# Window attention's probabilities transposed in two halves of the TensorE array, and the second image's first loads issued together

## The chip, the cores and the metric

The kernel runs on one core of a Trainium2 chip. The core has five engines that work side by side: TensorE (PE, matmuls; its weight loads are listed apart as PEld), VectorE (DVE), ScalarE (ACT), GpSimd (POOL) and SyncE (SP), which here issues nearly all the DMAs. The metric is the device time of one execution in microseconds. Before the change it was 1659.49 us, the median of three runs that took from 1656.48 to 1663.47 us.

## The reference

The input `x` is 16 images of 56 x 56 tokens with 128 channels, in float32. Two layers follow each other, both with a residual:

```python
# layer 0: shifted-window attention; 64 windows of 7 x 7 = 49 tokens, 4 heads of 32
x = x + L0_conv(_gn(x))            # group norm, qkv, dots * scale + bias + mask,
                                   # softmax over 49 keys, times v, w_out, b_out
# layer 1, on the 3136 tokens of an image in a row
t = t + L1_attn(_ln_t(t))          # causal linear attention: elu(q)+1, elu(k)+1, running sums
t = t + L1_ffn(_ln_t(t))           # batch norm, then y[t] = sigmoid(wx[t] + y[t-1] @ V.T)
```

The change lies in the first layer: in a window, `softmax(q k^T + bias + mask) @ v`.

## The kernel before, in words

The kernel goes over the 16 images, b = 0 to 15, and works on several at once. An image is cut twice. For the window attention it is eight rows of eight windows (`window_row`, u = 0 to 7, NW = 8 windows of WT = 49 tokens). For the linear attention and what follows it is six groups of 512 tokens and one of 64 (`token_group`, g = 0 to 6). The recurrent part of the feed-forward layer comes behind all images, from about 1500 us to the end, and the change doesn't touch it.

One window row is a chain of steps over the engines:

- ACT gathers the windows (`gather_windows`, L851); PE projects q and k (L864) and the values (L885); ACT copies them out.
- PE computes the scores (L909): 32 small matmuls per row, each with 32 rows of the array (a head) and 49 columns. The four heads lie on four strips of 32 rows. Head h's scores go to partitions 64 x (h mod 2) on, so that a partition half holds one head of a pair.
- DVE adds the mask and takes the maximum (L920, L932), POOL subtracts it (L935), ACT takes the exponential (L945), DVE sums (L949, L951), POOL scales (L954).
- PE transposes the probabilities (`turn`, L964). `p_buf` holds two heads in its two partition halves, rows 0 to 48 and rows 64 to 112, with two windows padded to 64 columns each beside each other. One transpose takes both halves at once: 113 rows, 128 columns. Eight transposes do a window row.
- ACT copies the transposed probabilities to `pT` (`turn_out`, L974), 904 elements per partition, of which the columns between the two heads are padding.
- PE multiplies with the values (`mix`, L983): 32 small matmuls, each with 49 rows in one of the two halves of the array and 32 columns. ACT writes the result to `oT` (`mix_out`, L1018).

The transposes, the scores and the mix each use one of two PSUM tiles, `pairs`, of two banks.

A float32 matmul appears in the trace as two matmul instructions, so 32 small matmuls are 64; a transpose appears as one.

The images' data come in twice. `load` brings the tokens as rows (`xt_bufs`, L323), for the residual. For images 1 to 15 `load_turned` and `load_blocks` bring the same image in four parts (q = 0 to 3) of blocks of 32 channels to `spare[0]` (L335); DVE turns these 32 x 32 blocks (`turn_rows`, L683), which gives the image with channels on partitions. Statistics (L755) and the group norm follow, and only then can the image's first window be gathered. Image 0 is transposed on PE instead (L649).

The order of the instructions on every engine is written by a planner (`Plan`), which runs in the kernel's own Python. Each step names its engine, a cost, a lag to its end, the steps it comes after and the buffers that it takes and drops. The planner plays the steps through with these numbers, forwards and backwards, many times, and emits them by start time in the best order it finds. The engines then run their queues in that order and wait on semaphores. A step whose `tiles` is set is one that uses a part of the array: having begun with such a step, the planner prefers another one nearby, and it adds 0.1 to the first of them (`SWITCH`). Before, `scores` and `mix` are marked so. SP's DMAs, too, stand in the planned order, so a DMA that waits holds those behind it.

In the planner's model the four parts of an image's blocks come after each other: each part's step names the part before it. This is a rule of the plan alone; no semaphore comes from it, since the parts write to different partitions.

## Time and profile before

| what | us |
|---|---|
| median of three runs | 1659.49 |
| the profiled execution | 1664.5 |
| its span on the core | 1661.4 |
| PE busy in the span | 1615.4 |
| DVE busy | 1398.1 |
| POOL busy | 1272.0 |
| ACT busy | 1183.5 |

The page of the profile gives the busy time of each engine, the chain of work that ended last followed back from the end, and the groups of instructions that cost most. In a group the first number is the time in which at least one of its instructions was under way, the second the mean duration of one in ns. On PE these durations overlap, since matmuls are pipelined: a step's price is better read in the order of time, from its first start to the first start of the step behind it. A stretch's busy times are read against its length. The granted clock is the share of TensorE's full clock, 1.00 for most of this execution.

### The profile page before, as it was taken

The page shows a single profiled execution, that of the slowest core. Times are in us where ns is not written, and L with a number is a line of the kernel's source. Part 1 is how long each engine was busy: PE and PEld are TensorE (multiplying, and loading weights), DVE is VectorE, ACT ScalarE, POOL GpSimd, SP SyncE. Part 2 cuts the span into 40 slices and gives each one's busy share as a digit, 9 for nine tenths or more (in the row PEclk, how much of TensorE's full clock was granted, in tenths as well). Part 3 has the DMA queues.
Part 4 walks back from the last instruction along what each step waited for, and adds up shares of the span by engine and source line. Part 5 has one row for each costly group of instructions (what it writes and reads, how often), then busy time and mean ns, then how long its engine had stood idle before and what let it go on. Part 6 is the DMA issues. An engine that isn't in the chain of part 4 may idle for free.

```text
span 1661.4 us, 63385 instructions
## 1 busy us (share of the span) xinstructions
PE 1615.4 (97%) x25458; PEld 1308.8 (79%) x25459; DVE 1398.1 (84%) x3044; ACT 1183.5 (71%) x3156; POOL 1272.0 (77%) x2154
## 2 busy tenths in 40 slices
PE   7899999999999999999999999999999999999997
PEld 6678787887878887878888778878888887876876
DVE  5779987897989888987979798978898786757997
ACT  5577776777777777777677777767677776766765
POOL 6788978897989898888989889878889786770000
PEclk9999999999999999999999999999999999999999
DMA  5486767677677768586766777776755655558999
GB/s 137 109 186 158 192 151 172 187 167 208 154 204 166 199 153 206 149 208 169 194 165 156 204 168 196 167 191 156 196 148 155 159 160 147 190 183 342 403 419 379
DMA packets 776720, 322.03 MB, mean 194 GB/s; under 512 B 400481, under 2 KB 760161, under 8 KB 774625
## 3 DMA queue, kind: packets, MB, share of 16 engines
q1 hardware_dynamic: 774832, 317.10, 69.9%
q8 instruction: 202, 3.31, 0.9%
q10 hardware_dynamic: 1584, 0.79, 0.2%
q14 instruction: 102, 0.83, 0.2%
HBM read 171.54 MB, written 146.24 MB: 191 GB/s over the span
## 4 chain that ended last, share of the span: by engine, by line
PE 69%; POOL 8%; DVE 7%; SPq 5%; DMA 5%; issue 3%; ACT 2%; DVEq 0%; POOLq 0%; ACTq 0%
PE bank L864 8%; PE bank L1269 8%; PE bank L885 5%; PE pair L909 5%; PE state_bank L1412 4%; PE pair L964 4%; PE pair L1401 4%; PE bank L1317 4%; PE pair L1404 4%; PE bank L1502 4%; PE bank L1372 4%; PE pair L983 4%; SPq L1072 4%; PE bank L1234 4%; PE z_buf L1785 2%
## 5 line engine op out<-in xcount | busy, mean ns | idle before, releaser
L954 POOL TENSOR_TENSOR p_buf<-p_buf,rc 128x784 f32<-128x784 f32 x128 | 194.4, 1519 | 42.7 <-DVE rc L951 14.2
L1269 PE MATMUL bank<-xnT,awc_sb 128*128 128x512 f32 (+1 forms) x448 | 212.9, 557 | 3.3 <-DVE xnT L1139 2.7
L935 POOL TENSOR_TENSOR s<-s,mx 128x784 f32<-128x784 f32 x128 | 192.2, 1502 | 30.8 <-DVE mx L932 28.5
L1279 ACT ACTIVATE r<-bank,bqk_neg 128x512 f32<-128x512 f32 (+1 forms) x224 | 143.4, 640 | 76.9 <-PE bank L1269 67.3
L1412 PEld LDWEIGHTS state_bank<-v_buf,k 128*128 128x128 f32 x768 | 125.4, 191 | 52.1 <-issue 26.7
L1292 DVE SCALAR_TENSOR_TENSOR f<-bank,bqk_one,r 128x512 f32<-128x512 f32 (+1 forms) x224 | 147.5, 658 | 12.6 <-ACT r L1288 12.1
L1412 PE MATMUL state_bank<-v_buf,k 128*128 128x129 f32 x768 | 155.4, 284 | 1.3 <-ACT state L1424 1.1
L974 ACT COPY pT<-pair 128x904 f32<-128x904 f32 x128 | 118.7, 927 | 51.0 <-PE pair L964 41.3
L1401 PE MATMUL pair<-state,f 128*128 128x129 f32 x768 | 153.1, 281 | 0.6 <-issue 0.6
L1424 ACT COPY state<-state_bank 128x129 f32<-128x129 f32 x384 | 107.0, 279 | 65.5 <-PE state_bank L1412 63.9
L1401 PEld LDWEIGHTS pair<-state,f 128*128 128x128 f32 x768 | 123.4, 192 | 37.0 <-issue 21.8
L920 DVE TENSOR_TENSOR s<-pair,wmask_sb 128x784 f32<-128x784 f32 x128 | 122.7, 958 | 34.2 <-PE pair L909 30.0
L909 PEld LDWEIGHTS pair<-kT,q_buf 32*49 32x49 f32 x8192 | 106.4, 121 | 41.9 <-issue 15.7
L949 DVE TENSOR_REDUCE sm<-p_buf 128x16 f32<-128x784 f32 x128 | 121.6, 950 | 18.6 <-ACT p_buf L945 18.3
L1223 POOL TENSOR_TENSOR xt_buf<-xt_buf,bout_sb 128x512 f32<-128x512 f32 (+1 forms) x112 | 129.1, 1158 | 10.7 <-DMA xt_buf<-in_x_dram 10.5
L1788 ACT ACTIVATE y_a<-z_buf,bsh 128x256 f32<-128x256 f32 (+1 forms) x218 | 103.0, 473 | 47.4 <-PE z_buf L1785 43.3
L1288 ACT ACTIVATE r<-r 128x512 f32<-128x512 f32 (+1 forms) x224 | 131.9, 589 | 2.4
L1785 PE MATMUL z_buf<-y_a,fvT_sb 128*128 128x256 f32 (+1 forms) x432 | 131.0, 389 | 0.4 <-ACT y_a L1788 0.4
L909 PE MATMUL pair<-kT,q_buf 32*49 32x49 f32 x8192 | 122.8, 206 | 2.8 <-issue 2.4
L964 PE MATMUL pair<-ident,p_buf 113*128 113x113 f32 x1024 | 120.9, 261 | 3.1 <-POOL p_buf L954 2.8
L964 PEld LDWEIGHTS pair<-ident,p_buf 113*128 113x128 f32 x1024 | 107.5, 142 | 20.5 <-issue 11.2
L932 DVE TENSOR_REDUCE mx<-s 128x16 f32<-128x784 f32 x128 | 121.5, 949 | 0.9
(170 smaller groups left out, 4697.1 us busy)
## 6 DMA issues: line engine op xcount, KB each, us to landing
x_d<-xt_buf SPq DMA_DIRECT2D x96, 256.0 KB, 2.6
xt_buf<-in_x_dram SPq DMA_DIRECT2D x93, 256.0 KB, 3.2
spare<-in_x_dram SPq DMA_DIRECT2D x60, 392.0 KB, 4.5
xs_d<-staged SPq DMA_DIRECT2D x15, 1568.0 KB, 6.9
xna_d<-spare SPq DMA_DIRECT2D x90, 256.0 KB, 2.7
xnk_d<-f SPq DMA_DIRECT2D x90, 256.0 KB, 3.0
xnf_d<-spare SPq DMA_DIRECT2D x90, 256.0 KB, 2.8
spare<-xna_d SPq DMA_DIRECT2D x256, 64.0 KB, 2.1
```

What stands on the lines that cost most here:

```text
L864: nc.tensor.matmul(d[key], wqkv_sb[:, j * P : (j + 1) * P], xk, start=True, stop=True)
L909: nc.tensor.matmul(sc[64 * hh : 64 * hh + WT, hp, w * WT : (w + 1) * WT], qT[r : r + HD, w * WT : (w + 1) * WT], d["kT"][r : r + HD, w * W ...
L935: nc.gpsimd.tensor_tensor(d["sf"], d["sf"], d["mx"].unsqueeze(2).to_broadcast([P, nb, WT]), ALU.subtract,)
L954: nc.gpsimd.tensor_tensor(prf, prf, d["rc"].unsqueeze(2).to_broadcast([P, nb, WT]), ALU.mult)
L964: nc.tensor.transpose(pt[:, hp, w2, 0:NQ2], pr[0:NQ2, hp, 2 * w2 : 2 * w2 + 2, :].rearrange("p w k -> p (w k)"), ident[0:NQ2, 0:NQ2],)
L1269: nc.tensor.matmul(d[f"p{j}"], awc_sb[:, j * P : (j + 1) * P], d["xT"][:, :nt], start=True, stop=True,)
L1279: nc.scalar.activation(d[f"r{j}"], d[f"p{j}"], AF.Relu, bias=bqk_neg[:, j : j + 1], scale=-1.0,)
L1288: nc.scalar.activation(d[f"r{j}"], d[f"r{j}"], AF.Exp, scale=-1.0)
L1292: nc.vector.scalar_tensor_tensor(d[key][:, :nt], d[f"p{j}"], bqk_one[:, j : j + 1], d[f"r{j}"], ALU.add, ALU.max,)
L1401: nc.tensor.matmul(to, chunk(d["f0"], cc), t["states"][c], start=True, stop=False)
L1412: nc.tensor.matmul(t["pd"], d["k"][:, cc, :], v1[:, cc, :], start=c == 0, stop=True, skip_group_check=True,)
L1785: nc.tensor.matmul(z, fvT_sb, y_prev, start=False, stop=True, skip_group_check=True)
```

## The change

In `turn` each head's probabilities are transposed by themselves. A transpose takes rows 0 to 48 or rows 64 to 112, and the identity's rows and columns of the same numbers, so that it uses one half of the array's rows; there are 16 per window row instead of 8, and the two halves alternate. Each half writes to a bank of its own of the `pair` tile. The result has 2 x 8 x 49 = 784 elements per partition without padding, and `pT`, its copy (`turn_out`) and the operand that `mix` reads are laid out accordingly. In the plan the transposes' cost goes from 0.77 to 0.40 and the copy's from 0.81 to 0.72, and the transposes are marked as `tiles`.

In `load_turned` the parts of image 1's blocks no longer come after each other in the plan; those of later images still do.

Since the planner orders everything by these numbers, the order of all engines' queues is another one after the change.

```diff
-        NQ2 = 64 + WT
...
-                        [issued, *parts[-1:]],
+                        [issued, *(parts[-1:] if b > 1 else [])],
...
             def turn():
-                pt = pairs[apt.place].rearrange("p h (w q) -> p h w q", w=NW // 2)
+                pt = pairs[apt.place][..., 0:UT].rearrange("p i (n q) -> p i n q", q=WT)
                 d["pt"] = pt
                 for hp in range(2):
                     for w2 in range(NW // 2):
-                        nc.tensor.transpose(
-                            pt[:, hp, w2, 0:NQ2],
-                            pr[0:NQ2, hp, 2 * w2 : 2 * w2 + 2, :].rearrange(
-                                "p w k -> p (w k)"
-                            ),
-                            ident[0:NQ2, 0:NQ2],
-                        )
+                        for hh in range(2):
+                            q = 64 * hh
+                            nc.tensor.transpose(
+                                pt[:, hh, NW // 2 * hp + w2, :],
+                                pr[q : q + WT, hp, 2 * w2 : 2 * w2 + 2, :].rearrange(
+                                    "p w k -> p (w k)"
+                                ),
+                                ident[q : q + WT, q : q + WT],
+                            )
 
             def turn_out():
-                d["pT"] = own(pT, P, 2, NW // 2, P)
-                nc.scalar.copy(d["pT"][..., 0:NQ2], d["pt"][..., 0:NQ2])
+                d["pT"] = own(pT, P, 2, NW, WT)
+                nc.scalar.copy(d["pT"], d["pt"])
...
-                                d["pT"][
-                                    a : a + WT, h // 2, w2, 64 * (h % 2) : 64 * (h % 2) + WT
-                                ],
+                                d["pT"][a : a + WT, h % 2, NW // 2 * (h // 2) + w2, :],
...
-            tu = st("PE", (0.77, 0.94), rank, turn, [m], takes=[apt])
-            last_turn[i % 2] = tu
-            tu = st("ACT", (0.81, 0.92), rank, turn_out, [tu], takes=[pT], drops=[apt])
+            tu = st("PE", (0.40, 0.50), rank, turn, [m], takes=[apt])
+            last_turn[i % 2] = tp = tu
+            tu = st("ACT", (0.72, 0.83), rank, turn_out, [tu], takes=[pT], drops=[apt])
             mi = st("PE", (0.74, 0.81), rank, mix, [tu, vo], takes=[apa], drops=[pT, v])
-            sc.tiles = mi.tiles = True
+            sc.tiles = mi.tiles = tp.tiles = True
```

## The prediction

> **What bounds the kernel now.** I read the page's chain of work first, then busy time by stretch, then the matmul and weight-load groups by form, and last the order in time of a few steady microseconds. The chain and the engine totals:

> ```profile
> PE 69%; POOL 8%; DVE 7%; SPq 5%; DMA 5%; issue 3%; ACT 2%; DVEq 0%; POOLq 0%; ACTq 0%
> PE 1615.4 (97%) x25458; PEld 1308.8 (79%) x25459; DVE 1398.1 (84%) x3044; ACT 1183.5 (71%) x3156; POOL 1272.0 (77%) x2154
> ```

> By stretch (columns: stretch, length, then busy PE, PEld, DVE, ACT, POOL, then granted clock, DMA share, GB/s):

> ```profile
> 41.50:83.00 41.50, 34.70 (x802) 27.06 (x801) 32.09 (x62) 22.86 (x55) 31.94 (x52) 0.96 0.45 108
> 124.50:1450.00 1325.50, 1312.77 (x22296) 1068.89 (x22296) 1138.51 (x2558) 968.63 (x2650) 1138.41 (x1916) 1.00 0.69 174
> ```

> From 124.5 to 1450 us PE is busy 99.0%, DVE and POOL 86%, ACT 73%. So in this stretch, where nearly all window work lies, a nanosecond of PE's own sequence is a nanosecond of the end, up to about 13% of slack on the next engines. In the stretch from 41.5 to 83 us PE stands idle for 6.8 us and its clock is 0.96, some 1.7 us more: image 0 runs out of work while image 1 isn't ready.

> The groups that the change touches and their nearest relatives, matmuls and then weight loads (mean ns after the busy time):

> ```profile
> L909 PE MATMUL pair<-kT,q_buf 32*49 32x49 f32 x8192 | 122.8, 206 | 2.8 <-issue 2.4 <-ACT raw L1482 0.4
> L964 PE MATMUL pair<-ident,p_buf 113*128 113x113 f32 x1024 | 120.9, 261 | 3.1 <-POOL p_buf L954 2.8 <-POOL spare L1111 0.3
> ...
> L1412 PEld LDWEIGHTS state_bank<-v_buf,k 128*128 128x128 f32 x768 | 125.4, 191 | 52.1 <-issue 26.7 <-ACT state L1424 3.9 <-ACT p_buf L945 1.2
> ...
> L964 PEld LDWEIGHTS pair<-ident,p_buf 113*128 113x128 f32 x1024 | 107.5, 142 | 20.5 <-issue 11.2 <-POOL p_buf L954 5.3 <-POOL gnb L814 0.5
> L909 PEld LDWEIGHTS pair<-kT,q_buf 32*49 32x49 f32 x8192 | 106.4, 121 | 41.9 <-issue 15.7 <-ACT state L1424 5.3 <-ACT r L1288 2.1
> ```

> These records overlap, so I price a step from its first start to the next step's first start, in PE's order of time:

> ```profile
> 707.08 0.94 PE L964 MATMUL pair<-ident,p_buf 113*128 113x113 f32 x8
> 707.86 0.84 PE L864 MATMUL bank<-x_buf,wqkv_sb 128*128 128x392 f32 x2
> ...
> 711.71 0.81 PE L983 MATMUL pair<-pT,v 49*32 49x49 f32 x64
> 712.45 0.95 PE L909 MATMUL pair<-kT,q_buf 32*49 32x49 f32 x64
> 713.33 0.93 PE L864 MATMUL bank<-oT_buf,wqkv_sb 128*128 128x392 f32 x2
> ...
> 722.64 0.39 PE L1412 MATMUL state_bank<-v_buf,k 128*128 128x129 f32 x2
> 722.87 0.39 PE L1404 MATMUL pair<-v_buf,raw 128*128 128x129 f32 x2
> 723.18 0.95 PE L909 MATMUL pair<-kT,q_buf 32*49 32x49 f32 x64
> 724.06 0.49 PE L1401 MATMUL pair<-state,f 128*128 128x129 f32 x2
> 724.39 0.39 PE L1404 MATMUL pair<-v_buf,raw 128*128 128x129 f32 x2
> 724.61 0.59 PE L1269 MATMUL bank<-xnT,awc_sb 128*128 128x512 f32 x1
> ```

> Three prices follow. Eight transposes take 0.78 us (0.775 is the median over the trace), 97 ns each, 0.86 ns for each of 113 columns. Scores take 0.88, mix 0.74. And a matmul pair that takes 0.23 takes 0.31 ahead of scores, and the first pair after scores takes 0.33: an excursion from whole-array matmuls into tiles and back costs 0.09 + 0.10, about 0.195 us. Mix followed by scores pays nothing between them.

> **The transposes.** 128 steps of 8 become 128 steps of 16, each with 49 moving columns in one half of the rows. The trace has no half-array transpose. The nearest row is scores: 49 moving columns too, one column tile to a row strip, 64 instructions on four strips, so 16 rounds. At 0.86 ns a column a round streams 42 ns; 16 x 42 = 0.68 us, and 0.20 of the 0.88 is start and drain. The new step is 8 rounds of two halves: 8 x 42 + 200 = 0.54 us. Best case: no start and drain, 0.34. Worst cases: the weight load sets the round. A transposed load of 128 columns records 142 ns against 121 for 49 ordinary and 191 for 128 ordinary columns; along that line (0.89 ns a column) it streams about 66 ns, so 8 x 66 + 200 = 0.73; and if the load can't hide behind the same half's stream, 8 x 108 + 200 = 1.06. I take 0.54, because scores has loads of 44 ns by the same line and streams of 42, and yet does a round in 55 ns, start and drain counted in: 128 x (0.54 - 0.775) = **-30.1 us**.

> [...]

> **The switches.** The old transposes ran on the whole array; the new ones are a tile mode. In the built programs' order of instructions, before has 212 excursions into tiles (84 lone scores, 84 lone mixes, 44 pairs); after has 315, 109 of them transposes all alone and 19 transposes beside scores or mix. 103 more at 0.195 us: **+20.1 us**. Bounds: 0 if a half-row mode needed no drain, and 3.7 more if the 19 pay between modes too.

> **The copy-out and mix.** The copy falls from 904 to 784 elements, 921 to some 800 ns, 15 us less on ACT. ACT is at 73%, and PE's matmuls of mix waited 1.6 us in all for it: nothing, and no loss either. Mix reads the same number of elements; the two banks belong to the same pair as before, so no buffer is added.

> **The blocks of image 1.** Before, SP issues its four loads at 11.7, 18.2 (two) and 52.6 us; the last stands behind stores and read-backs of image 0, and DVE turns the first blocks at 68.2:

> ```profile
> 52.58 0.43 SPq L335 DMA_DIRECT2D spare<-in_x_dram  x1
> 68.16 1.16 DVE L683 STREAM_TRANSPOSE xw_buf<-spare 128x448 f32<-128x448 f32 x2
> ```

> After, all four stand ahead of image 1's seven group loads, and DVE turns the first two after image 0's third window mask and maximum (36.7 to 37.7 us in this trace). Image 1's first projection stands 68th on PE instead of 98th, among image 0's windows. Its work fills holes between 41.5 and 83 us, worth at most 6.8 + 1.7 = 8.5 us. What is late next are image 0's own softmax rounds, which still leave holes; I take **-5**, between -8.5 and +5.7. The loss: image 1's group loads are issued after three more block loads (two took 3.8 us, so 5.7), and POOL's bias adds on them, ahead of image 0's masks in its queue, start at 31.6. Loads issued by 18.1 and landing 5 us later have 8 us to spare, which covers it. SP issues the same instructions in number; image 2's paced loads move up, ahead of image 0's first store and read-back, and cost SP under 1 us each, inside the same -5.

> **Sum.** -30.1 + 20.1 - 5 = -15 us. The profiled execution took 1664.5 us (span 1661.4), 5 above the median of the runs, 1659.5. So 1649.5 against its own time, 1644.5 against the median. No change, as far as a measurement of this kernel can tell, is within 0.5%, 8.3 us.

> **Rivals.**
> Load-bound rounds: 0.73 us a step, -5.8 + 20.1 and the start between 0 and -5, so 1669 to 1674. For it: the loads double while streams shorten. Against it: the line through ordinary loads may overstate a transposed one.
> Loads not hidden, the other sign: in one half, load and stream alternate, 1.06 us at each transpose, +36.5 + 20.1 - 5, 1711. It decides from 0.66 us a step on, where the sum is zero. For it: mix, on the same 64-row halves, needs 92 ns a round for 49 columns. Against it: mix loads four column tiles in each half, the transposes one.
> The end doesn't follow PE: POOL and DVE at 86% would have to set the pace; 1% of PE can't make that so on average, but the planner writes a new order whose holes differ by some us. Then -2 or so, 1657.
> The start gets worse instead of better: +5.7 and -10 from the rest, 1655.

> **How the numbers follow.** Forecast 0.58, load-bound 0.15, not hidden 0.12, end not following 0.08, start worse 0.07. The forecast's own range: steps of 0.44 (half of scores) with -8.5 give 1628; steps of 0.60 with 0 give 1657. Faster: 0.53 of the 0.58. Slower: the 0.12 and most of the 0.15. The range 1626 to 1674 leaves out the unhidden loads and a little at the low end.

> **What would show it.** Right: the transposes' line x2048, 0.5 to 0.6 us from their first start to the next step's; about 0.1 us more on either side of a lone one; the copy-out near 0.8 us; image 1's blocks turned before 45 us, PE busier than 34.7 in 41.5 to 83. Wrong: transposes of 0.66 us or more, a load mean well above 142 ns, or PE idle on POOL in the steady stretch.

## The result and the profile after

The changed kernel took 1664.21 us in the median of five runs (1660.32 to 1668.67), the kernel before 1656.49 us beside it (1655.40 to 1663.47). The ratio is 1.0042, with a 95% interval from 1.0023 to 1.0061: a loss of some 7 us where 15 us of gain were forecast. On another chip the ratio was 1.0013 (0.9993 to 1.0033). The kernel is at best as fast as it was.

The profiled execution of the changed kernel is the fastest of the five, 1660.32 us with a span of 1658.5. So its trace tells what single steps cost, but not the loss; that needs the experiments. First the page's chain of work and engine totals of the changed kernel:

```profile
PE 78%; DVE 6%; SPq 4%; DMA 4%; POOL 4%; issue 3%; ACT 1%; DVEq 0%; POOLq 0%
PE 1608.7 (97%) x26483; PEld 1285.2 (77%) x26483; DVE 1402.0 (85%) x3044; ACT 1177.0 (71%) x3156; POOL 1271.7 (77%) x2154
```

PE carries still more of the chain. The groups by line and form (busy time and mean ns of one, then the idle time just before them) give the transposes:

```profile
L965 PE MATMUL pair<-ident,p_buf 49*128 49x49 f32 x2048 | 89.7, 228 | 1.9 <-POOL p_buf L953 1.7 <-POOL xt_buf L600 0.2
```

their weight loads:

```profile
L965 PEld LDWEIGHTS pair<-ident,p_buf 49*128 49x128 f32 x2048 | 73.7, 138 | 35.1 <-issue 10.2 <-POOL spare L1110 2.8 <-POOL s L934 2.8
```

and on the page the copy-out:

```profile
L975 ACT COPY pT<-pair 128x784 f32<-128x784 f32 x128 | 104.4, 816 | 40.3 <-PE pair L965 35.8
```

The copy-out takes 0.82 us as forecast. The loads' records are as long as before, 138 against 142 ns. What a step costs stands in PE's order of time in the changed kernel (start, duration, form):

```profile
700.25 0.70 PE L965 MATMUL pair<-ident,p_buf 49*128 49x49 f32 x16
700.88 1.16 PE L1371 MATMUL bank<-f,f 128*128 128x128 f32 x8
...
707.19 0.82 PE L863 MATMUL bank<-oT_buf,wqkv_sb 128*128 128x392 f32 x2
707.85 1.02 PE L1268 MATMUL bank<-xnT,awc_sb 128*128 128x512 f32 x2
708.80 0.70 PE L965 MATMUL pair<-ident,p_buf 49*128 49x49 f32 x16
709.43 0.93 PE L863 MATMUL bank<-x_buf,wqkv_sb 128*128 128x392 f32 x2
710.20 1.05 PE L884 MATMUL bank<-wqkv_sb,oT_buf 128*128 128x128 f32 x8
711.08 0.39 PE L1411 MATMUL state_bank<-v_buf,k 128*128 128x129 f32 x2
711.40 0.81 PE L984 MATMUL pair<-pT,v 49*32 49x49 f32 x64
712.14 0.95 PE L908 MATMUL pair<-kT,q_buf 32*49 32x49 f32 x64
```

From 700.25 to 700.88 and from 708.80 to 709.43 a transpose step takes 0.63 us; the median over the trace is 0.627, against 0.775 before and 0.54 forecast. The step after a lone one pays as forecast: the projection at 709.43 needs 0.77 where the one at 707.19 needs 0.66 without a switch, and the pair at 711.08 needs 0.32 instead of 0.23 ahead of a mix. Within a step the two halves' matmuls start 3 ns apart, and the next two follow 62 ns later, but 99 ns after the first two, and the next step starts 155 ns after the last two: 99 + 6 x 62 + 155 = 626 ns from the first start to the next step (medians over the trace).

The start did better than forecast. Of the changed kernel, the same stretches as before (length, then busy PE, PEld, DVE, ACT, POOL, then clock, DMA share, GB/s):

```profile
41.50:83.00 41.50, 38.71 (x1002) 30.07 (x1000) 34.59 (x69) 29.46 (x68) 40.06 (x58) 1.00 0.58 137
83.00:124.50 41.50, 41.50 (x788) 34.03 (x786) 38.47 (x84) 30.92 (x83) 35.87 (x65) 1.00 0.70 148
124.50:1450.00 1325.50, 1307.58 (x23007) 1045.22 (x23008) 1132.76 (x2539) 959.73 (x2643) 1132.64 (x1906) 1.00 0.69 174
```

In the order of time (start, duration), image 1's loads on SP's queue:

```profile
11.98 6.42 SPq L335 DMA_DIRECT2D spare<-in_x_dram  x4
```

and DVE's first turns of them:

```profile
36.98 1.16 DVE L682 STREAM_TRANSPOSE xw_buf<-spare 128x448 f32<-128x448 f32 x2
```

All four loads are out by 18.4 us, DVE turns the first blocks at 37.0 instead of 68.2, and PE is busy 38.7 of the 41.5 us instead of 34.7. In the steady stretch PE is idle for 17.9 us instead of 12.7.

To see where time goes I split PE's time up to the recurrent part in two, the same way for every trace. A step's price is the lower quartile, over the twelve full runs, of the time from its first start to the next step's, taken per form, count and tile neighbours. The sum of prices is what PE's own work and its switches need; the rest is stalls and time at half clock. The sums of prices depend on how steps are grouped: other groupings move them by up to 3 us against each other, so smaller differences between them carry nothing. In the table "clock" is the mean granted clock over all of a kernel's timed runs, while the split is from its one trace.

| kernel | excursions | prices, us | rest, us | of it 41.5 to 124.5 | clock | ratio to before (interval) |
|---|---|---|---|---|---|---|
| before | 212 | 1436.4 | 56.9 | 13.0 | 0.9955 | |
| changed | 315 | 1438.5 | 50.1 | 4.0 | 0.9912 | 1.0042 (1.0023 to 1.0061) |
| changed, again | 315 | 1438.4 | 64.8 | 6.7 | 0.9903 | 1.0013 (0.9993 to 1.0033) |
| halves alone | 317 | 1440.2 | 63.2 | 12.5 | 0.9898 | 1.0061 (1.0043 to 1.0078) |
| loads alone | 203 | 1434.9 | 68.3 | 5.6 | 0.9952 | 1.0048 (1.0028 to 1.0069) |
| halves, old order | 332 | 1442.4 | 56.2 | 10.8 | 0.9945 | 1.0040 (1.0025 to 1.0055) |
| whole, new order | 206 | 1434.8 | 52.4 | 4.1 | 0.9938 | 0.9982 (0.9961 to 1.0004) |
| the same again | 206 | 1434.8 | 62.8 | 4.3 | 0.9931 | 0.9997 (0.9980 to 1.0014) |
| honest plan | 295 | 1434.8 | 63.9 | 6.0 | 0.9940 | 1.0002 (0.9987 to 1.0017) |
| loads, switch 0.2 | 201 | 1434.5 | 51.7 | 4.7 | 0.9957 | 0.9943 (0.9925 to 0.9961) |
| near 8, switch 0.3 | 183 | 1430.9 | 65.0 | 7.2 | 0.9933 | 1.0035 (1.0021 to 1.0049) |
| before, switch 0.2 | 202 | 1434.7 | 59.8 | 14.8 | 0.9953 | 1.0011 (0.9994 to 1.0028) |

### The profile page after: what moved, and what is told of

The parts are those of the page before. It is cut to its first block, busy times and chain, and to the rows that moved or that the text cites. A ratio compares the mean times of both kernels' runs of the same rounds, so it can differ in the third digit from the quotient of the medians.

```text
span 1658.5 us, 65427 instructions
## 1 busy us (share of the span) xinstructions
PE 1608.7 (97%) x26483; PEld 1285.2 (77%) x26483; DVE 1402.0 (85%) x3044; ACT 1177.0 (71%) x3156; POOL 1271.7 (77%) x2154
## 3 DMA queue, kind: packets, MB, share of 16 engines
q8 instruction: 210, 3.44, 0.9%
## 4 chain that ended last, share of the span: by engine, by line
PE 78%; DVE 6%; SPq 4%; DMA 4%; POOL 4%; issue 3%; ACT 1%; DVEq 0%; POOLq 0%
PE bank L1268 10%; PE bank L863 9%; PE bank L884 6%; PE pair L908 6%; PE state_bank L1411 5%; PE bank L1316 5%; PE pair L1400 5%; PE bank L1371 5%; PE pair L984 5%; PE bank L1233 5%; PE pair L1403 5%; PE bank L1501 5%; PE pair L965 4%; SPq L1071 3%; DVE z_buf L1772 2%
## 5 line engine op out<-in xcount | busy, mean ns | idle before, releaser
L1411 PEld LDWEIGHTS state_bank<-v_buf,k 128*128 128x128 f32 x768 | 123.6, 191 | 41.9 <-issue 24.1
L1411 PE MATMUL state_bank<-v_buf,k 128*128 128x129 f32 x768 | 156.1, 285 | 0.0
L1787 ACT ACTIVATE y_a<-z_buf,bsh 128x256 f32<-128x256 f32 (+1 forms) x218 | 103.1, 473 | 45.6 <-PE z_buf L1784 41.5
L975 ACT COPY pT<-pair 128x784 f32<-128x784 f32 x128 | 104.4, 816 | 40.3 <-PE pair L965 35.8
L1316 PEld LDWEIGHTS bank<-awc_sb,xnT 128*128 128x128 f32 x800 | 101.1, 192 | 23.0 <-issue 11.8
L1316 PE MATMUL bank<-awc_sb,xnT 128*128 128x128 f32 x800 | 112.3, 281 | 6.0 <-issue 3.8
```

Of the source, the lines that this page charges most:

```text
L1316: nc.tensor.matmul(pv[:, cc, :], chunk(d["xT"], cc), awc_sb[:, 2 * P : 3 * P], start=True, stop=True,)
L1411: nc.tensor.matmul(t["pd"], d["k"][:, cc, :], v1[:, cc, :], start=c == 0, stop=True, skip_group_check=True,)
```

## The experiments

The theory after the result was a ledger (A): the steps cost 0.627 us, the switches eat that saving, and the start gains. Two rivals: the clock (B), that is, more stretches at half clock; and the order (C), that is, stalls that depend on what the planner happened to write.

### The parts apart, and code and order crossed

The half-array transposes with their plan entries, without the change to the loads:

```diff
-                        [issued, *(parts[-1:] if b > 1 else [])],
+                        [issued, *parts[-1:]],
```

> Only the half-array transposes with their plan entries; image 1's blocks keep their chain in the plan. In the built order there are 317 excursions into tiles, against 212 before and 315 in the changed kernel. Theory A, a ledger of PE's own time: a transpose step costs 0.627 us instead of 0.775 (128 x -0.148 = -18.9), each further excursion 0.195 (105 x 0.195 = +20.5), so +1.6 us against before, 1.001. Rival B, the clock: half-array transposes bring more half-clock windows of 3.4 us, each worth 1.7 us; then +6 to +12 and a mean clock at or under 0.991. Rival C, the order: what the planner happens to write decides, and no sum of steps gives the time; then anything within 10 us of before.

Measured: 1673.67 us, ratio 1.0061, mean clock 0.9898. That is 9 us more than the ledger allows, and the clock is as low as rival B said.

The loads alone, in the kernel before:

```diff
-                        [issued, *parts[-1:]],
+                        [issued, *(parts[-1:] if b > 1 else [])],
```

> Only the loads of image 1 without the chain; the transposes are those of before. 203 excursions against 212; image 1's first projection is the 68th row on PE instead of the 98th. Theory A: -5 from the holes between 41 and 125 us, 9 x -0.195 = -1.8, so about -7 us, 0.996. Rival B: the same, -5 to -9, with a clock of 0.994 or more. Rival C: the gain at the start is lost again in the order behind it, 0 or worse.

Measured: 1672.15 us, ratio 1.0048. The start gained as in the changed kernel (rest of 5.6 us instead of 13.0), and the prices fell by 1.5, but between 124.5 and 1440 us the rest grew from 29 to 47 us. This is rival C, at the clock of before: same work, a better start, and another order that loses 17 us to stalls.

The half-array transposes in the order of before, and the whole-array ones in the order of the changed kernel. Only the code of the transposes, their copy and mix's operand is exchanged; the plan is that of the other kernel:

```diff
# halves, old order: the changed kernel with the plan of before
-                        [issued, *(parts[-1:] if b > 1 else [])],
+                        [issued, *parts[-1:]],
...
-            tu = st("PE", (0.40, 0.50), rank, turn, [m], takes=[apt])
+            tu = st("PE", (0.77, 0.94), rank, turn, [m], takes=[apt])
...
-            tu = st("ACT", (0.72, 0.83), rank, turn_out, [tu], takes=[pT], drops=[apt])
+            tu = st("ACT", (0.81, 0.92), rank, turn_out, [tu], takes=[pT], drops=[apt])
...
-            sc.tiles = mi.tiles = tp.tiles = True
+            sc.tiles = mi.tiles = True
```

> The half-array transposes in exactly the order of before: the plan has before's costs, marks and chain, and only the transposes, their copy and mix's operand are the changed ones. 332 excursions, 120 more than before. Theory A: 128 x -0.148 + 120 x 0.195 = -18.9 + 23.4 = +4.5 us, 1.003, at the clock of before. Rival B: +10 or more, with a lower clock than before. Rival C: the order is that of before, so the time is within 1.5 us of before.

Measured: 1669.58 us, ratio 1.0040 (1.0025 to 1.0055), 6.6 us more than before; clock 0.9945 against 0.9953. The prices rose by 6.0 and the rest stayed. With the order held still, theory A holds: the half-array transposes cost time by themselves, through 120 more excursions (+23.4) that outweigh the shorter steps (-18.9).

The other half of the crossing, the kernel before with the plan of the changed one:

```diff
# whole, new order
-                        [issued, *parts[-1:]],
+                        [issued, *(parts[-1:] if b > 1 else [])],
...
-            tu = st("PE", (0.77, 0.94), rank, turn, [m], takes=[apt])
-            last_turn[i % 2] = tu
-            tu = st("ACT", (0.81, 0.92), rank, turn_out, [tu], takes=[pT], drops=[apt])
+            tu = st("PE", (0.40, 0.50), rank, turn, [m], takes=[apt])
+            last_turn[i % 2] = tp = tu
+            tu = st("ACT", (0.72, 0.83), rank, turn_out, [tu], takes=[pT], drops=[apt])
...
-            sc.tiles = mi.tiles = True
+            sc.tiles = mi.tiles = tp.tiles = True
```

> The whole-array transposes of before in exactly the order of the changed kernel: the plan has the changed costs, marks and loads. 206 excursions. Theory A: -5 at the start and 6 x -0.195 from the excursions, -6 us, 0.996, though the order was made for steps of 0.40. Rival B: the same, with a clock of 0.994 or more. Rival C: the order carries the loss, so the time is that of the changed kernel, +6 to +8.

Measured: 1661.25 us, ratio 0.9982 (0.9961 to 1.0004), and the same program, run again on another chip, 1664.17 us and 0.9997 (0.9980 to 1.0014), with this expectation:

> The whole-array transposes in the order of the changed kernel once more, which stood at 0.998 with an interval of 0.996 to 1.0004. If its start gain of 8 us and six excursions fewer carry to the end, 0.995 to 0.999 and faster than before beyond the interval; if the earlier result was chance, 1.000 or more. Its clock should again lie above the changed kernel's 0.990 if the half-array transposes in this order are what brings the half-clock windows.

So the order of the changed kernel with the old transposes is level with before or a little faster. Set against the changed kernel's 1.0042 and 1.0013, the transposes cost in the new order, too: 1.0028 against 0.9990 in the mean of two, though the pair 1.0013 and 0.9997 alone wouldn't show it. The 8 us of the start don't reach the end in full: the two traces of this one program differ by 10.4 us in the rest.

### What sets a transpose's pace

Fewer stationary columns, in the changed kernel:

```diff
-                                pt[:, hh, NW // 2 * hp + w2, :],
+                                pt[0:96, hh, NW // 2 * hp + w2, :],
...
-                                ),
+                                )[:, 0:96],
```

> The changed kernel, but each transpose takes only 96 of the 128 stationary columns (the last 32 key columns of every second window are left out, so pT keeps old values there); order and moving columns are the same. If the weight load sets the transposes' round of 62 ns, the round falls toward 50 and the step from 0.627 to 0.52 us or so; if the 49 moving columns or the issue set it, the step stays at 0.62 to 0.63.

More moving columns:

```diff
-                pt = pairs[apt.place][..., 0:UT].rearrange("p i (n q) -> p i n q", q=WT)
+                pt = pairs[apt.place].rearrange("p i (n q) -> p i n q", q=64)
...
-                                pr[q : q + WT, hp, 2 * w2 : 2 * w2 + 2, :].rearrange(
+                                pr[q : q + 64, hp, 2 * w2 : 2 * w2 + 2, :].rearrange(
...
-                                ident[q : q + WT, q : q + WT],
+                                ident[q : q + 64, q : q + 64],
...
-                nc.scalar.copy(d["pT"], d["pt"])
+                nc.scalar.copy(d["pT"], d["pt"][..., 0:WT])
```

> The changed kernel, but each transpose streams 64 moving columns instead of 49 (the 15 more rows hold padding that the copy skips); stationary columns and order are the same. If the weight load sets the round, the step stays within 0.02 of 0.627 us, since 64 columns stream in 55 ns; if the stream sets it, a round grows by 13 ns and the step to 0.73.

PE's order of time with 96 stationary columns:

```profile
442.67 0.58 PE L965 MATMUL pair<-ident,p_buf 49*96 49x49 f32 x16
443.18 0.49 PE L1411 MATMUL state_bank<-v_buf,k 128*128 128x129 f32 x2
```

and with 64 moving columns:

```profile
443.72 0.71 PE L965 MATMUL pair<-ident,p_buf 64*128 64x64 f32 x16
444.36 0.49 PE L1411 MATMUL state_bank<-v_buf,k 128*128 128x129 f32 x2
```

The two took 1662.50 and 1666.63 us in one execution each, which says nothing beside the spread of single runs. The step falls to 0.51 us (0.515 in the median) with a quarter fewer columns to load, and stays at 0.64 with a third more to stream. So the weight load sets the round here: 0.112 us over 8 rounds and 32 columns is 0.44 ns a column, and at that price, as an estimate, 128 columns need 56 of the round's 62 ns. The mean record of a load agrees: 125 ns for 96 columns and 139 for 128 in these two traces, again 0.44 ns a column. Among the transposes the rows hardly show in it: with 128 columns it is 138 ns for 49 rows (the changed kernel), 139 for 64 and 142 for 113 (before).

### Prices in the plan, and order as such

The changed kernel with measured prices:

```diff
-    SWITCH = 0.1
+    SWITCH = 0.2
...
-            tu = st("PE", (0.40, 0.50), rank, turn, [m], takes=[apt])
+            tu = st("PE", (0.63, 0.70), rank, turn, [m], takes=[apt])
```

> The changed kernel with measured prices in the plan: 0.63 (lag 0.70) for the transposes instead of 0.40 (0.50), and 0.2 instead of 0.1 for a switch into tiles. 295 excursions instead of 315. Theory A: 20 x -0.195 = -3.9 us against the changed kernel, about 0.998 of it, and more if its stalls came from an order made for steps that are too short. Rival C, the order is luck: anything within 10 us of the changed kernel, also slower.

The changed kernel unedited, beside it:

> The changed kernel itself once more, beside before on the same chip, so that it can be compared with the other four orders. Theory A (PE's own time, plus a start that gains 9 us): 18.9 off for the steps, 20.1 on for 103 more excursions, 9 off at the start, so 0.995 at equal clock. Theory B (the clock): again a mean clock near 0.991 against 0.995, some 6 us of extra half-clock time, which cancels the gain: 1.000 to 1.005, and slower executions have the lower clocks.

Measured side by side: 1667.78 us with measured prices and 1666.58 for the changed kernel, ratios 1.0002 and 1.0013, which can't be told apart. The prices fell by 3.6 as reckoned and the clock rose from 0.9903 to 0.9940, but the time didn't follow. The rest is 63.9 us in the one trace and 64.8 in the other, though up to the recurrent part 13.7 us of it ran at half clock instead of 30.7: other delays took that place, and one trace each doesn't tell which. And since the same transposes run here at 0.9940 and in the old order at 0.9945, the low clock doesn't come from the half-array transposes alone.

The kernel before with another order, as a control, and two orders for the old transposes with the loads unchained:

```diff
# before, switch 0.2; the second also has the loads without the chain
-    SWITCH = 0.1
+    SWITCH = 0.2
```

> The kernel before with 0.2 instead of 0.1 for a switch into tiles and nothing else: a control for what another order does to the same work. 202 excursions. The ledger: 10 x -0.195 = -2 us, 0.999. If order is luck, it lands up to 10 us away from that, with steady-stretch stalls to match, in spite of a sum that says no change.

> The whole-array transposes and image 1's loads without the chain, as in the run with the loads alone, but with 0.2 instead of 0.1 for a switch into tiles: another order for the same work, 201 excursions. The ledger: 11 x -0.195 = -2.1 against before and some -8 at the start, 0.994. Order is luck: the run with the loads alone had the same two gains and was 0.5% slower through stalls in the steady stretch, so anything from 0.993 to 1.006.

```diff
# near 8, switch 0.3: whole-array transposes, loads without the chain
-    SWITCH = 0.1
-    NEAR = 3.0
+    SWITCH = 0.3
+    NEAR = 8.0
```

> The whole-array transposes, image 1's loads without the chain, 0.3 for a switch into tiles, and the planner may take a tile step that lies up to 8 instead of 3 behind: 183 excursions, 29 fewer than before. The ledger: 29 x -0.195 = -5.7 and -8 at the start, 0.992. If stalls in the order decide instead, 1.000 or more.

Measured: 1666.35, 1655.69 and 1669.25 us, ratios 1.0011, 0.9943 and 1.0035. The control is level with before. The kernel with the loads unchained and 0.2 for a switch is the fastest of all, 1655.69 us against 1663.86 for before, beyond the interval. The one with the lowest sum of prices, 5.5 us under before, is slower than before. Between the runs with the loads alone and with the switch at 0.2, the work is the same and the prices differ by 0.4 us; the ratios, each to before on its own chip, are 1.0048 and 0.9943. So an order is worth some 17 us here, more than all that the change's terms add up to. Which order turns out well no sum of prices foretold: that is luck.

### What the rest is made of

PE's order of time in the changed kernel around one stall, then busy times in stretches ahead of, in and behind it:

```profile
190.37 0.95 PE L908 MATMUL pair<-kT,q_buf 32*49 32x49 f32 x64
191.24 0.81 PE L984 MATMUL pair<-pT,v 49*32 49x49 f32 x64
191.98 0.49 PE L1316 MATMUL bank<-awc_sb,xnT 128*128 128x128 f32 x2
196.28 1.11 PE L1316 MATMUL bank<-awc_sb,xnT 128*128 128x128 f32 x6 [3.81 <-issue]
197.18 1.91 PE L1268 MATMUL bank<-xnT,awc_sb 128*128 128x512 f32 x2
```

```profile
188.00:192.00 4.00, 4.00 (x157) 3.28 (x155) 2.25 (x6) 3.82 (x11) 3.04 (x8) 1.00 1.09 369
192.50:196.20 3.70, 0.00 (x0) 0.00 (x0) 1.05 (x2) 1.00 (x5) 1.76 (x2) 1.00 1.06 306
196.60:200.00 3.40, 3.40 (x13) 2.37 (x12) 1.57 (x2) 0.84 (x2) 0.93 (x1) 0.51 0.63 173
```

PE stands for 3.8 us in the middle of four equal matmuls, waiting for no semaphore that the profile shows, while the DMA engines are full (shares of 1.09 and 1.06). Then it runs for 3.4 us at half clock: the 512-column pair at 197.18 takes 1.91 us, against 1.02 elsewhere. In the second trace of the same program PE stands at the same place:

```profile
196.99 0.49 PE L1316 MATMUL bank<-awc_sb,xnT 128*128 128x128 f32 x2
200.85 0.83 PE L1316 MATMUL bank<-awc_sb,xnT 128*128 128x128 f32 x6 [3.37 <-issue]
201.51 1.02 PE L1268 MATMUL bank<-xnT,awc_sb 128*128 128x512 f32 x2
```

This time no half clock follows. Over all fourteen traces' steady stretches every half-clock stretch came behind a stall of 1.5 us or more; of 44 stalls between 1.0 and 1.5 us none was followed by one, of the 56 longer ones 30 were.

Other long stalls wait for data: at 1384.19 PE had stood 3.47 us for `xnT`, whose blocks go to DRAM and back, and in the second trace 4.05 us at the same place. In the twelve runs of the changed kernel time goes with the clock, 1.46 us for 0.001 (correlation -0.84); one window at half clock is 0.001 of the mean clock and 1.7 us of work, so the two agree. Its clock lies 0.0052 under that of before beside it, which is 7.6 us.

## Why the prediction was wrong

**Transposes, -30.1.** This is the term that was mis-sized most: it measured -18.9, so 11.2 us of the forecast gain weren't there. The pace follows the weight load, which was the first rival. I reasoned that loads hide behind streams. Here they do, since a round of 62 ns has no room for a load of 56 and a stream of 42, both estimates, one after the other; but the loads are the longer of the two, and a round takes 62 ns instead of 42. Scores couldn't tell me: its loads, 44 ns by my line, are hardly longer than its streams of 42, so its rounds don't show what a longer load does. The line through the load records gave 66 ns (65 when reckoned again) and was near the truth, and the same 142 ns record already stood in the table of before. My fixed 0.20 us for start and drain was too high (626 - 8 x 62 = 130 ns), which hid part of the miss: with the rounds of 62 ns it would have given 0.70 us.

**Switches, +20.1.** Right in count and price: 0.09 to 0.10 on either side. In the changed kernel's steady stretch the pair of L1411, 0.22 us without a switch, takes 0.318 ahead of transposes and 0.326 behind them, and 0.317 and 0.326 ahead of and behind scores or mix (medians): this half-row mode pays on either side what the other two tile modes pay. With the real step the two terms sum to +1.2, and in the old order to +4.5, where 6.6 was measured.

**Copy and mix, 0.** The copy took 0.82 us; mix kept its 0.74. Nothing speaks against it.

**Image 1's blocks, -5.** The mechanism was right, and the size too small for the stretch, -9.0 and -6.3 in the two traces. That it carries to the end isn't shown: the loads alone made the kernel slower.

**The end follows PE.** This is the step that turned a small gain into a loss: with the transposes at -18.9 the sum would still have been -4 us. It failed in its use. I took "a nanosecond of PE's own sequence is a nanosecond of the end" for a sum of steps across two different orders. With the order fixed it holds: +6.0 in prices, +6.6 in time. Across orders it doesn't, and the sum put the new order's stalls and half clock at nothing: the rival that gave the planner's new holes "some us" was too small by several times, since orders of equal work differ by 17 us and single traces of one program by 15.

**What closes the sum, and what stays open.** Prices +2.1 and the start -6 to -9 would have made the changed kernel some 4 to 7 us faster. Its lower clock, 7.6 us by the slope, and the steady stretch's stalls take that back; measured were +2 to +7. How much falls to each isn't shown, since the slope has the stalls that bring the half clock in it. The order lowers the clock by itself (0.9938 and 0.9931 against 0.9953 and 0.9956 of before beside it); the transposes in the old order hardly do (0.9945 against 0.9953, within the spread); both together come to 0.9903, clearly lower than either. Why the half-array transposes lower the clock further in this order stays open: from 124.5 to 1440 us PE is idle for 17.6 and 23.9 us in the two traces of the changed kernel, and for 17.8 and 22.1 with the old transposes in its order. The recurrent part, which the change doesn't touch, took 1.3 to 1.8 us longer in these four traces than in that of before; the sum had no term for it.

## What to carry to other kernels

Splitting a transpose over row halves shortened the stream here (49 moving columns instead of 113, matmul records of 228 ns instead of 261) but not the weight load, which keeps all 128 stationary columns (records of 142 and 138 ns): price a small tiled step by the longer of the two, and add the switch, 0.195 us here, on both sides of every lone one. A step that gains 0.15 us by a tile mode and pays 0.195 for standing alone loses. In the changed kernel's steady stretch twelve transpose steps stand between scores and whole-array work; they take 0.627 us as the others do, and the scores 0.88, so nothing is paid between the two. By these prices such a mode gains where its steps stand beside other tile steps; no run had all of them so. Where a planner rewrites the whole order, compare the new code in the old order first; the order alone moved this kernel by 1%, and one run of a new order says nothing of the edit that caused it.

## What was not expected of the hardware

PE's waits named "issue" go with the packets of the instruction queue. That queue (packets, MB, share) in the kernel before:

```profile
q8 instruction: 202, 3.31, 0.9%
```

and of the changed one:

```profile
q8 instruction: 210, 3.44, 0.9%
```

The 0.13 MB more for 2049 more PE instructions (1025 matmuls and 1024 weight loads; DVE, ACT and POOL have as many as before) is some 64 bytes each, so as an estimate about 256 PE instructions go to a packet of 16 KB (3.44 MB in 210). In six traces, 40 of 46 issue stalls over 0.3 us had such a packet under way in the stall or at most 3 us ahead of it; the other six were the one near 11 us. That alone says little, since a moment picked at random has such a packet as near in two cases of three. The end of the stall says more: in all fourteen traces each of the 92 issue stalls over 0.3 us (without the one near 11 us) ended 1.20 to 1.64 us after such a packet had landed, which is so for 6% of random moments. A score step and a mix side by side are 256 instructions in 1.6 us, and the stalls of 3.8 and 3.4 us above follow just such a pair. Such stalls took 2.5 us of the steady stretch in the trace of before and 1.4 in the fastest kernel's, but 7 to 11 in all traces with half-array transposes, and in three with the old ones (8.0 to 8.7); the other two have 2.3 and 4.0. In the stall of 3.8 us, from 192.47 to 196.28, the packet began at 193.80 and took 0.88 us, against 1.00 in the median of the trace's 210: it wasn't slow, and why it didn't begin earlier isn't shown.
